# A graph network on one NeuronCore: one gathered tile in four blocks is fetched row by row by SyncE, with addresses from its registers

## The chip, the core and the metric

The kernel runs on one core of a Trainium2 chip, in one launch. The metric is the device time of an execution in microseconds (us), the median of several runs. The program before the change was timed three times: 7339.11, 7335.75 and 7313.08 us, median 7335.75 us. One more execution was profiled.

The engines are called as the profile calls them: PE (matrix multiply; PEld is its weight load), DVE (vector), ACT (scalar), POOL (the engine that issues gathers here) and SP (SyncE, which only issues DMAs). "SPq" is a line of SP's queue. L653 means line 653 of the kernel.

## What is computed

There are 10000 nodes of 512 features and 160000 edges sorted by destination. Layer 0 gives every edge one of four types; layer 1 is two plain neighbourhood averages. Cut to what matters:

```
h   = relu(layernorm(x))
msg = (h @ rel_W[r] + rel_b[r])[src, edge_type]          # one row of 512 per edge
agg = segment_sum(msg, dst) / max(deg, 1)
x1  = layernorm(h + h @ self_W + self_b + agg)
x   = x + layernorm(x1 + gelu(x1 @ W1 + b1) @ W2 + b2)   # layer 0
h   = relu(layernorm(x))
h   = relu(h @ W_self1 + mean(h[src] over edges) @ W_neigh1 + b1)
h   = relu(h @ W_self2 + mean(h[src] over edges) @ W_neigh2 + b2)
out = x + h                                              # layer 1
```

All is float32. What costs time is that a row of 2 KB has to be fetched from DRAM for every edge, three times over: once from the table `hall_d` of all four products of every node, once from `h1_d` and once from `h2_d`.

## The kernel before, in words

Nodes are handled in blocks of 128, one on each partition: 78 full blocks and one last of 16 nodes (`NB` = 79, `full` = 78). The program has four passes, which follow each other.

**Pass 1** (`products`, L597) normalises x, multiplies it by the five weight matrices of layer 0 and stores `hall_d`. Beside it a generator, `edges` (L562), works out on DVE which rows each block needs. It yields between its steps, and `products` resumes it once a block. `lists` (L391) writes index tables that stay in SBUF.

**The index tables.** A node's first T = 11 incoming edges are its own lanes: gather t of block b takes for partition p the t-th edge of node p (`row`), and the gathered tile is simply added to the block's sum. The edges beyond the eleventh are packed, 128 to a tile, and each block has five such tiles (`orow`, `OT` = 5). What does not fit in these goes to tiles shared by several blocks: one for every 4 blocks and one for every 16 (`SPANS` = (4, 16), L80). `srow[0]` and `srow[1]` (L127) hold their row numbers, one column for a tile, 128 partitions deep; `share` (L534) fills a column once the last block of its span has been looked up. Which node a packed row belongs to is in `loc`; `hots` (L666) turns that into 0/1 matrices with which PE adds the rows to the right partitions.

**Passes 2, 3 and 4** (`aligned`, L636) loop over the blocks in the order 78, 0, 1, ..., 77. The order of instructions on each engine is that in which they are written (`manual_schedule`). For every block:

- `gather` (L649) has POOL issue one indirect DMA for each tile, 128 rows of 2 KB: at every fourth block the tile of 4 blocks and at every sixteenth that of 16 (L658 to L660, called `tail0` and `tail1`, two buffers each), then five `orow` tiles, then eleven `row` tiles. The last sixteen share a ring of 28 buffers (`RING`, L640).
- `sums` (L674) has PE add the seven packed tiles into a PSUM tile `pa`, through the 0/1 matrices. The order (L678) begins with `tail1`, then `tail0`, then the five `orow` tiles; matmuls are at L680.
- `add` (L688) has DVE add the eleven `row` tiles to `pa`, one by one (L692).

`begin` (L684) is gather and sums for the next block, called while the current one is worked on. So POOL runs ahead of PE and DVE until the ring is full, and a ring buffer comes free when PE or DVE has used it.

Pass 2 (loop from L903) then normalises the block and gives it to a two-matrix MLP that is done by groups of four blocks, spread over the following iterations (`Group.parts`). SP loads `xs` (L719, two blocks at a time) and `xr` (L725) and stores `h1` (L859) and `xn` (L878). Passes 3 and 4 (loop from L1004) are the two averages: ACT scales the sum, PE transposes it and multiplies by two matrices (L1018, L984), DVE adds bias and residual. SP loads `hb`, 1 MB for four blocks (L970), in pass 4 also `res` (L973), and stores `ob` (L997), also 1 MB for four blocks. SP issues nothing else there, and it waits in the order of the program: a load that needs a buffer or a store that needs a result holds up what is behind it.

Between passes 2 and 3, L944 shifts all row numbers right by two, from rows of `hall_d` (node and type) to rows of `h1_d` and `h2_d` (node).

The functions the change touches:

Of the kernel before, what the change touches and what calls it, by code (L numbers as in the profile page):

```python
# [8 lines left out]
F32 = mybir.dt.float32  # L9
F32R = mybir.dt.float32r  # L10
BF16 = mybir.dt.bfloat16
I32 = mybir.dt.int32
# [9 lines left out]
def kernel(  # L22
# [101 lines left out]

    row = const.tile([P, full, T], I32, name="row")
    orow = const.tile([P, NB, OT], I32, name="orow")
    srow = [const.tile([P, -(-full // n)], I32, name=f"srow{i}") for i, n in enumerate(SPANS)]  # L127
    loc = const.tile([P, NB, OT + NL], F32, name="loc")
    fits = const.tile([1, 1], I32, name="fits")
# [261 lines left out]
    def lists(ep, ep2, pse, found):  # L391
# [166 lines left out]
        while ahead:  # L558
            look_up(*ahead.pop(0))
            yield  # L560

    def edges(ep, ep2, pse):  # L562
        found = {k: ep.tile([P, NB], F32, name=f"f_{k}") 
# [72 lines left out]
    def aligned(ctxa):  # L636
# [8 lines left out]
            return min(P, N - b * P)  # L645

        tails = [None] * NL

        def gather(b, table):  # L649

            def rows(n, idx, name="rows", bufs=RING):
                t = gat.tile([P, D], F32, name=name, bufs=bufs)
                nc.gpsimd.indirect_dma_start(  # L653
                    out=t[:n], out_offset=None, in_=table,
                    in_offset=bass.IndirectOffsetOnAxis(ap=idx, axis=0))
                return t[:n]

            for lv, n in enumerate(SPANS):  # L658
                if b < full and b % n == 0:
                    tails[lv] = rows(P, srow[lv][:, b // n:b // n + 1], f"tail{lv}", 2)  # L660
            others = [rows(P, orow[:, b, t:t + 1]) for t in range(OT if b < full else OT_LAST)]
            if b < full:
                others += tails
            return others, [rows(P, row[:, b, t:t + 1]) for t in range(own(b))]
# [9 lines left out]
        def sums(b, others, hot):  # L674

            r, n = height(b), len(others)
            pa = psA.tile([P, D], F32, name="pa")
            order = list(range(n)) if b == full else list(range(OT, n))[::-1] + list(range(OT))  # L678
            for t in order:
                nc.tensor.matmul(pa[:r], hot[:, t, :r], others[t], start=(t == order[0]),  # L680
                                 stop=(t == order[-1]))
            return pa
# [12 lines left out]
        with ExitStack() as s:  # L695
# [209 lines left out]
            for bs in plan:  # L905
                for b in bs:
                    r = height(b)
                    if b == bs[0]:
                        before, grp = grp, Group(bs)
                    if i + 2 < len(blocks):  # L910
                        load(blocks[i + 2])
                    if i + 1 < len(blocks):
                        hot = hots(blocks[i + 1])
                    got = second()
                    pa, mine = held
                    add(b, pa, mine)
                    v = nodes[b]
                    nc.vector.scalar_tensor_tensor(v[:r], pa[:r], rdeg[:r, b:b + 1], v[:r],
                                                   op0=OP.mult, op1=OP.add)
                    first = (b, now.stats(v[:r], r))  # L920
                    part = products(queue.pop(0) if queue else [], turning)
                    next(part)
                    now.finish()
                    scaled(got, first)
                    next(part, None)
                    if i + 1 < len(blocks):
                        held = begin(blocks[i + 1], hot, table)

                    if b == bs[0] and before:
                        queue += before.parts()  # L930
                    turning = lambda g=grp, b=b, v=v: g.turn(b, v)
                    i += 1
# [8 lines left out]
                next(part, None)  # L941


        for t in (row, orow, *srow):  # L944
            nc.vector.tensor_scalar(t, t, R.bit_length() - 1, None, op0=OP.logical_shift_right)
        quads = [[full]] + [rest[i:i + 4] for i in range(0, full, 4)]
        place = {b: (q, c) for q, bs in enumerate(quads) for c, b in enumerate(bs)}
        for step, (h_d, ws, wn, bs) in enumerate(((h1_d, ws1, wn1, bs1), (h2_d, ws2, wn2, bs2))):
            with ExitStack() as s:
                wp = s.enter_context(tc.tile_pool(name="wp3", bufs=1))  # L950
                ip = s.enter_context(tc.tile_pool(name="ip", bufs=2))
                psT = s.enter_context(tc.tile_pool(name="psT3", bufs=3, space=PSUM))
                psO = s.enter_context(tc.tile_pool(name="psO3", bufs=3, space=PSUM))
                wss = wp.tile([P, KC, D], F32, name="wss")
                wns = wp.tile([P, KC, D], F32, name="wns")
                nc.sync.dma_start(wss, ws.rearrange("(k p) n -> p k n", p=P))
                nc.sync.dma_start(wns, wn.rearrange("(k p) n -> p k n", p=P))
                bss = wide(wp, bs, D, "bss")
                hbs, ress, outs, hTs = {}, {}, {}, {}

                def quad(t, q, name, bufs):

                    b, n = quads[q][0], len(quads[q])
                    return (ip.tile([P, 4, D], F32, name=name, bufs=bufs)[:height(b), :n],
                            rows_of(t, (b, n, height(b))))

                def load(q):
                    if q < len(quads):
                        hbs[q], at = quad(h_d, q, "hb", 2)
                        nc.sync.dma_start(hbs[q], at)  # L970
                        if step:
                            ress[q], at = quad(xn_d, q, "res", 3)
                            nc.sync.dma_start(ress[q], at)  # L973

                def turn(b):
                    q, c = place[b]
                    hTs[b] = ip.tile([P, KC, P], F32, name="hTb")
                    transposed(psT, hTs[b][:, :, :height(b)], hbs[q][:, c, :], height(b))

                def finish(b, po, mT):  # L980
                    r = height(b)
                    q, c = place[b]
                    for k in range(KC):
                        nc.tensor.matmul(po[:r], mT[:, k, :r], wns[:, k, :], start=False,  # L984
                                         stop=(k == KC - 1))
                    if c == 0:
                        outs[q] = quad(out if step else h2_d, q, "ob", 2)
                    o = outs[q][0][:, c, :]
                    if step:
                        nc.vector.tensor_tensor(po[:r], po[:r], bss[:r], op=OP.add)  # L990
                        nc.vector.scalar_tensor_tensor(o, po[:r], 0.0, ress[q][:, c, :],
                                                       op0=OP.max, op1=OP.add)
                    else:
                        nc.vector.tensor_tensor(o, po[:r], bss[:r], op=OP.add)  # L994
                        nc.scalar.activation(o, o, AF.Relu)
                    if b == quads[q][-1]:
                        nc.sync.dma_start(outs[q][1], outs[q][0])  # L997

                load(0)
                load(1)  # L1000
                turn(blocks[0])
                before = None
                held = begin(blocks[0], hots(blocks[0]), h_d)
                for i, b in enumerate(blocks):  # L1004
                    r = height(b)
                    q, c = place[b]
                    if q and c == 0:
                        load(q + 1)
                    if i + 1 < len(blocks):
                        hot = hots(blocks[i + 1])  # L1010
                    pa, mine = held
                    add(b, pa, mine)
                    m = ip.tile([P, D], F32, name="mb")
                    nc.scalar.activation(m[:r], pa[:r], AF.Copy, scale=rdeg[:r, b:b + 1])  # L1014
                    po = psO.tile([P, D], F32, name="po3")
                    hT = hTs.pop(b)
                    for k in range(KC):
                        nc.tensor.matmul(po[:r], hT[:, k, :r], wss[:, k, :], start=(k == 0),  # L1018
                                         stop=False)
                    if before:  # L1020
                        finish(*before)
                    if i + 1 < len(blocks):
                        turn(blocks[i + 1])
                        held = begin(blocks[i + 1], hot, h_d)
                    mT = ip.tile([P, KC, P], F32, name="mTb")
                    transposed(psT, mT[:, :, :r], m[:r], r)
                    before = (b, po, mT)
                finish(*before)
# [308 lines left out]
```

## Time and profile before

| what | value |
|---|---|
| median of the three runs | 7335.75 us |
| the profiled execution: its own time | 7342.91 us |
| its span, first to last instruction | 7341.1 us |
| POOL busy in the span | 3792.5 us, 52%, 3927 instructions |
| PE / DVE / ACT busy | 77% / 50% / 14% |
| DMA queue of POOL (q0) | 308768 packets, 1008.91 MB, 46.5% of 16 engines' span |
| DMA queue of SP (q1) | 134034 packets, 262.10 MB, 10.1% |
| pass 1 | 0 to 1612 us |
| pass 2, first to last gather | 1612 to 3498 us |
| rest of the MLP, then pass 3, first to last gather | 3498 to 3621; 3621 to 5447 us |
| pass 4, first to last gather, then the end | 5479 to 7308; to 7341 us |

A page of such a profile has the busy time of each engine, the span in 40 slices, the DMA queues, the chain of work that ended last, and the costliest groups of instructions. "Busy" leaves out register, branch, semaphore and DMA-issuing instructions, so SP has no busy time at all and its work is to be seen only in the timeline of its queue. A group's line gives engine, operation, what it writes and reads, how many there are, their mean in ns, and the idle time of the engine just before them with what ended most of it. "Issue" is idle time that no recorded event explains; "remote" is a wait ended by something that the records don't name.

### The profile page before, as it was taken

The page shows a single profiled execution, that of the slowest core. Times are in us where ns is not written, and L with a number is a line of the kernel's source. Part 1 is how long each engine was busy: PE and PEld are TensorE (multiplying, and loading weights), DVE is VectorE, ACT ScalarE, POOL GpSimd, SP SyncE. Part 2 cuts the span into 40 slices and gives each one's busy share as a digit, 9 for nine tenths or more (in the row PEclk, how much of TensorE's full clock was granted, in tenths as well). Part 3 has the DMA queues.
Part 4 walks back from the last instruction along what each step waited for, and adds up shares of the span by engine and source line. Part 5 has one row for each costly group of instructions (what it writes and reads, how often), then busy time and mean ns, then how long its engine had stood idle before and what let it go on. Part 6 is the DMA issues. An engine that isn't in the chain of part 4 may idle for free.

```text
span 7341.1 us, 49909 instructions
## 1 busy us (share of the span) xinstructions
PE 5665.5 (77%) x14251; PEld 2553.8 (35%) x14251; DVE 3658.8 (50%) x7297; ACT 1016.3 (14%) x1667; POOL 3792.5 (52%) x3927
## 2 busy tenths in 40 slices
PE   6999999986889889899766666766665666666666
PEld 3444444432334334344323332332322333332232
DVE  5347777424666666666334434443333444443444
ACT  1000000002232233233201100110100000000000
POOL 0000000016666666666266666666656666666665
PEclk9999999997999999999878888888887888888888
DMA  3222222236767777777366666666666777777775
GB/s 141 109 97 98 93 104 92 85 135 194 211 205 224 224 221 225 220 227 225 129 198 206 206 209 204 208 204 206 203 196 208 220 216 216 219 217 214 220 219 169
DMA packets 456992, 1361.46 MB, mean 185 GB/s; under 512 B 71746, under 2 KB 71746, under 8 KB 446578
## 3 DMA queue, kind: packets, MB, share of 16 engines
q0 software_dynamic: 308768, 1008.91, 46.5%
q1 hardware_dynamic: 134034, 262.10, 10.1%
q10 hardware_dynamic: 13904, 87.17, 3.0%
q8 instruction: 114, 1.87, 0.1%
q14 instruction: 172, 1.41, 0.1%
HBM read 1150.89 MB, written 207.01 MB: 185 GB/s over the span
## 4 chain that ended last, share of the span: by engine, by line
PE 39%; issue 20%; another core or an unknown queue 17%; ACT 3%; DVE 3%; DMA 1%; POOL 1%; ACTq 0%; POOLq 0%; DVEq 0%; SPq 0%
PE pa L680 11%; PE ph L776 6%; PE pm L613 6%; PE po L787 6%; PE po L984 4%; PE po L1018 4%; DVE pa L692 2%; PE pT L167 1%; POOL rows L653 1%; ACT hTb L168 1%; ACT mTb L168 1%; ACT mb L1014 0%; PE pT L764 0%; ACT hid L778 0%
## 5 line engine op out<-in xcount | busy, mean ns | idle before, releaser
L692 DVE TENSOR_TENSOR pa<-pa,rows 128x512 f32<-128x512 f32 x2574 | 1798.5, 699 | 1002.9 <-issue 689.3
L653 POOL DMA_INDIRECT rows<-h_d,row x1716 | 1663.6, 969 | 929.1 <-issue 428.5
L984 PE MATMUL po<-wns,mTb 128*128 128x512 f32 (+1 forms) x1264 | 704.5, 709 | 587.5 <-issue 310.2
L680 PE MATMUL pa<-rows,hot 128*128 128x512 f32 (+1 forms) x2358 | 1080.7, 605 | 46.1 <-issue 20.6
L653 POOL DMA_INDIRECT rows<-hall_d,row x858 | 849.8, 990 | 504.4 <-issue 193.7
L613 PE MATMUL pm<-wrel,hT 128*128 128x512 f32 (+1 forms) x2528 | 1098.1, 592 | 0.0
L1018 PE MATMUL po<-wss,hTb 128*128 128x512 f32 (+1 forms) x1264 | 700.6, 706 | 475.6 <-ACT hTb L168 387.3
L653 POOL DMA_INDIRECT rows<-h_d,orow x786 | 754.1, 959 | 400.1 <-issue 220.7
L776 PE MATMUL ph<-x1T,w1s 128*128 128x512 f32 (+2 forms) x1344 | 606.1, 605 | 158.9 <-ACT hid L778 111.4
L613 PEld LDWEIGHTS pm<-wrel,hT 128*128 128x128 f32 (+1 forms) x2528 | 477.0, 189 | 605.8 <-issue 595.3
L680 PEld LDWEIGHTS pa<-rows,hot 128*128 128x128 f32 (+1 forms) x2358 | 454.2, 193 | 641.9 <-issue 603.7
L984 PEld LDWEIGHTS po<-wns,mTb 128*128 128x128 f32 (+1 forms) x1264 | 280.8, 228 | 995.9 <-issue 691.6
L653 POOL DMA_INDIRECT rows<-hall_d,orow x393 | 373.1, 949 | 434.8 <-SPq L1333 308.5
L787 PE MATMUL po<-w2s,hid 128*128 128x512 f32 (+1 forms) x1264 | 561.4, 596 | 23.2 <-issue 20.8
L1018 PEld LDWEIGHTS po<-wss,hTb 128*128 128x128 f32 (+1 forms) x1264 | 273.7, 228 | 846.3 <-ACT hTb L168 440.4
L680 PE MATMUL pa<-tail,hot 128*128 128x512 f32 x936 | 457.7, 607 | 53.3 <-issue 49.2
L990 DVE TENSOR_TENSOR po<-po,bss 128x512 f32<-128x512 f32 (+1 forms) x79 | 55.0, 696 | 811.3 <-remote 702.7
L487 POOL DMA_INDIRECT win<-rec_d,at x79 | 74.8, 947 | 727.9 <-issue 637.1
L776 PEld LDWEIGHTS ph<-x1T,w1s 128*128 128x128 f32 x1344 | 263.8, 204 | 470.7 <-issue 332.1
L616 DVE TENSOR_TENSOR ha<-pm,brel 128x512 f32<-128x512 f32 (+1 forms) x316 | 216.4, 687 | 405.1 <-PE pm L613 405.1
L994 DVE TENSOR_TENSOR ob<-po,bss 128x512 f32<-128x512 f32 (+1 forms) x79 | 54.4, 688 | 597.4 <-remote 268.8
L787 PEld LDWEIGHTS po<-w2s,hid 128*128 128x128 f32 (+1 forms) x1264 | 236.2, 190 | 312.5 <-issue 308.0
(233 smaller groups left out, 4171.5 us busy)
## 6 DMA issues: line engine op xcount, KB each, us to landing
hall_d<-ha ACTq DMA_DIRECT2D x78, 1024.0 KB
hb<-h_d SPq DMA_DIRECT2D x38, 1024.0 KB
rows<-h_d,row POOLq DMA_INDIRECT x1716
xs<-xs_d SPq DMA_DIRECT2D x39, 512.0 KB
xr<-xr_d SPq DMA_DIRECT2D x39, 512.0 KB
xn_d<-xr SPq DMA_DIRECT2D x39, 512.0 KB
h_d<-h SPq DMA_DIRECT2D x39, 512.0 KB
xg<-in_x_dram SPq DMA_DIRECT2D x19, 1024.0 KB
```

What stands on the lines that cost most here:

```text
L167: nc.tensor.transpose(p[:, k, :r], rows[:, k * P:(k + 1) * P], ident[:r, :r])
L168: nc.scalar.copy(dest, p[:, :, :r])
L487: nc.gpsimd.indirect_dma_start(out=win[:, c, :], out_offset=None, in_=rec_d, in_offset=bass.IndirectOffsetOnAxis(ap=at[:, c:c + 1], axis=0))
L613: nc.tensor.matmul(pm[:r], hT[:, k, :r], w[:, k, :], start=(k == 0), stop=(k == KC - 1))
L616: nc.vector.tensor_tensor(ha[:r, j - 1, :], pm[:r], brel[:r, (j - 1) * D:j * D], op=OP.add)
L653: nc.gpsimd.indirect_dma_start(out=t[:n], out_offset=None, in_=table, in_offset=bass.IndirectOffsetOnAxis(ap=idx, axis=0))
L680: nc.tensor.matmul(pa[:r], hot[:, t, :r], others[t], start=(t == order[0]), stop=(t == order[-1]))
L692: nc.vector.tensor_tensor(pa[:r], pa[:r], t[:r], op=OP.add)
L776: nc.tensor.matmul(ph[:, :n], w1s[:, k, f * P:(f + 1) * P], self.xT[:, k, :n], start=(k == 0), stop=(k == KC - 1))
L787: nc.tensor.matmul(po[:r], self.hid[:, f, c * r:(c + 1) * r], w2s[:, f, :], start=(f == 0), stop=(f == FC - 1))
L984: nc.tensor.matmul(po[:r], mT[:, k, :r], wns[:, k, :], start=False, stop=(k == KC - 1))
L1018: nc.tensor.matmul(po[:r], hT[:, k, :r], wss[:, k, :], start=(k == 0), stop=False)
```

## The change

Except for the first of a pass, the tiles that four blocks share are no longer gathered by POOL. A transposed copy of `srow[0]`, called `srow_1`, has one tile's 128 row numbers in one partition. It is made at the end of `lists`, by a copy to float, a PE transpose and a copy back to integers, and L944 shifts it with the other tables.

`fetch(b, table)` is called at the head of every iteration of all three loops, after the iteration's `load`. In the four iterations of one span it fetches the tile of the next: each call loads 32 row numbers into 32 registers of SP with one load instruction, and then issues 32 DMAs on SP, one a row, each with its source address computed from a register. A row is written as four pieces of 128 floats. It does nothing for the last, short block and from the span on that doesn't exist. So it works in 76 iterations of each pass, for spans 1 to 19.

`gather` takes the fetched tile instead of gathering one, and `sums` takes `tail1` first, then the five `orow` tiles, and `tail0` last.

```diff
+    srow_1 = const.tile([-(-full // SPANS[0]), P], I32, name="srow_1")
...
         while ahead:
             look_up(*ahead.pop(0))
             yield
+        ns = srow_1.shape[0]
+        srow_f = ep.tile([P, ns], F32, name="srow_f")
+        nc.vector.tensor_copy(srow_f, srow[0])
+        pl = pse.tile([P, 512], F32, name="pe")
+        nc.tensor.transpose(pl[:ns, :P], srow_f, ident)
+        nc.vector.tensor_copy(srow_1, pl[:ns, :P])
...
+        coming = {}
+        regs = [nc.sync.alloc_register(f"row{i}") for i in range(P // SPANS[0])]
+
+        def fetch(b, table):
+
+            span, part = b // SPANS[0] + 1, b % SPANS[0]
+            if b == full or span * SPANS[0] >= full:
+                return
+            if part == 0:
+                coming[span] = gat.tile([P, D], F32, name="tail0", bufs=2)
+            p0 = part * len(regs)
+            nc.sync.load(regs, srow_1[span:span + 1, p0:p0 + len(regs)])
+            for i, reg in enumerate(regs):
+                at = nc.sync.snap(reg, min_val=0, max_val=table.shape[0] - 1)
+                nc.sync.dma_start(
+                    coming[span][p0 + i:p0 + i + 1, :].rearrange("p (c d) -> p c d", c=4),
+                    table[bass.ds(at, 1), :].rearrange("p (c d) -> p c d", c=4))
...
-                    tails[lv] = rows(P, srow[lv][:, b // n:b // n + 1], f"tail{lv}", 2)
+                    tails[lv] = coming.pop(b // n) if b and not lv else rows(P, srow[lv][:, b // n:b // n + 1], f"tail{lv}", 2)
...
-            order = list(range(n)) if b == full else list(range(OT, n))[::-1] + list(range(OT))
+            order = list(range(n)) if b == full else [n - 1, *range(n - 1)]
...
                     if i + 2 < len(blocks):
                         load(blocks[i + 2])
+                    fetch(b, table)
...
-        for t in (row, orow, *srow):
+        for t in (row, orow, srow_1, *srow):
...
                     if q and c == 0:
                         load(q + 1)
+                    fetch(b, h_d)
```

## The prediction, made before the changed kernel ran

> **What bounds the kernel now.** I read the passes' busy times first, then POOL's timeline, then POOL's waits in each pass, and last SP's queue, since the change moves work from POOL to SP. The first view is busy time by stretch, from the first to the last gather of passes 2, 3 and 4.
>
> ```profile
> core 0: us, PE busy (x) PEld busy (x) DVE busy (x) ACT busy (x) POOL busy (x), PEclk, DMA share, GB/s
> 1612.00:3498.00 1886.00, 1601.41 (x3768) 705.52 (x3769) 1177.75 (x1952) 536.10 (x862) 1247.33 (x1275) 0.91 0.72 220
> 3621.00:5446.00 1825.00, 1219.87 (x2931) 546.08 (x2932) 711.37 (x992) 178.10 (x308) 1222.68 (x1275) 0.83 0.69 206
> 5480.00:7307.00 1827.00, 1210.86 (x2932) 542.84 (x2933) 763.29 (x1068) 135.22 (x232) 1238.20 (x1275) 0.81 0.71 217
> ```
>
> A pass has about 1276 gathers in 79 blocks: 23.9 us a block in pass 2 and 23.1 in passes 3 and 4. POOL looks two thirds busy, but its timeline says more:
>
> ```profile
> 6039.58 0.94 POOL L653 DMA_INDIRECT rows<-h_d,row  x1 [0.30 <-issue]
> 6040.82 0.94 POOL L653 DMA_INDIRECT rows<-h_d,row  x1 [0.30 <-issue]
> 6042.07 0.94 POOL L653 DMA_INDIRECT rows<-h_d,row  x1 [0.30 <-issue]
> 6043.32 0.94 POOL L653 DMA_INDIRECT tail<-h_d,srow  x1 [0.30 <-DMA rows<-h_d,row]
> ...
> 6058.30 0.95 POOL L653 DMA_INDIRECT rows<-h_d,row  x1 [0.30 <-issue]
> 6064.77 0.94 POOL L653 DMA_INDIRECT rows<-h_d,row  x1 [5.52 <-remote]
> ```
>
> A gather starts every 1.25 us, 0.95 of it shown busy and 0.30 not. 1276 x 1.25 = 1595 us: POOL issues back to back for 85% of pass 2 and 87% of passes 3 and 4. The rest is stalls like that at 6058, about 290 us in pass 2 and 230 in each of the others, where POOL wants a ring buffer that PE or DVE hasn't freed. POOL's waits in pass 2 (total us, times, longest us) name PE, and PE is busy 1601 of 1886 us there, so pass 2 is nearly as much PE's as POOL's.
>
> ```profile
> POOL rows L653 <- PE pa L680: 141.3, 42, 13.4
> POOL rows L653 <- PE po L787: 41.2, 34, 3.3
> ```
>
> SP's queue, in pass 3 and at the start of pass 2:
>
> ```profile
> 4017.19 0.36 SPq L970 DMA_DIRECT2D hb<-h_d  x1
> 4064.39 0.36 SPq L997 DMA_DIRECT2D h_d<-ob  x1
> 4110.15 0.36 SPq L970 DMA_DIRECT2D hb<-h_d  x1
> ...
> 1611.01 0.36 SPq L140 DMA_DIRECT2D ln1w<-in_L_gnn_ln_w_dram  x1
> 1611.49 0.35 SPq L140 DMA_DIRECT2D lnb<-in_L_gnn_ln_b_dram  x1
> 1611.95 0.36 SPq L741 DMA_DIRECT2D h<-in_L_gnn_b_dram  x1
> ```
>
> SP issues two DMAs in four blocks and waits otherwise. Back to back, one takes 0.36 us and the next starts 0.46 later; over the 100 closest pairs of the trace the spacing is 0.37 to 0.57 us, median 0.41 to 0.45.
>
> **What the Trainium skill says.** "Perfetto Trace Analysis", section "DMA Instruction — HWDGE (DVE, Sync)": the recorded duration of such a DMA is the sequencer's and the descriptor generator's time, without the data. The trace agrees: 0.36 us for an `hb` load whose last landing comes 4.6 to 5 us after issue, with its first packet 1.0 us after issue. So 0.36 is a price for SP's time. "DMA: Bandwidth & Descriptors", section "Why a DMA increments its semaphore by 16 and not by 1": a DMA runs on the largest number of engines, up to 16, that divides its outermost dimension, on SP's path the lowest-numbered ones. A row cut in four would use engines 0 to 3; no run here shows it yet. "Runtime: NRT & Kernel Launch", section "Instruction fetch mechanics": a register load costs about 200 ns a register even in bulk (from HBM, in its account). The trace has only loads of one register, 0.47 us on SP (L1300).
>
> **The change, part by part.** (1) *Removed:* 19 gathers in each of three passes, 57 x 1.25 = 71 us of POOL's time. (2) *Added on SP:* 76 fetches in a pass, each a load of 32 registers and 32 DMAs. The trace shows neither a bulk load nor an address from a register. The load is bounded by 0.47 us (as one register) and 32 x 0.2 = 6.4 us (the page's price); I take 2.5, since a row of one partition ought to come in fewer trips than 32. A row's DMA is bounded below by the closest spacing, 0.41 us, and above by twice that, 0.82, for a few register operations, the bounds of the address and the 12 increments that four engines don't make. I take 0.55. One fetch F is then 2.5 + 32 x 0.55 = 20 us, with ends at 0.5 + 13.1 = 13.6 and 6.4 + 26.2 = 33 us. A block gives 23.1 us (23.9 in pass 2). SP's own DMAs are under 0.5 us a block, and DMAs behind a 1 MB load may wait some 5 us for it, once or twice in four blocks, another 1 to 2 us a block. So SP fits at F = 20 with 1 to 2 us to spare, and stops fitting at F of about 22 to 23, that is 0.62 us a row. Everything hangs on that. (3) *Waits:* a fetch at iteration b stands ahead of that iteration's stores and, in pass 2, of `xr` and the next `xs`; each may come up to 20 us later than now. They hide behind their buffers: `xs` is loaded two blocks ahead, `hb` four, `xr` is used an iteration later. In passes 3 and 4 SP leaves the `ob` store in the middle of iteration b (b divisible by 4), issues three fetches in 60 us, and the last must have landed for the sums in iteration b+3, 69 us after the store: 7 us to spare, allowing 2 for landing. If SP is later, PE waits, and DVE, ACT and POOL's ring behind it. (4) *Order of the matmuls:* `tail0` last costs nothing by itself and gives it five tiles of 2 x 0.43 us, 4 us, more time. (5) *DMA load:* a fetched tile puts 64 KB on each of engines 0 to 3 in place of 16 KB on all; in four blocks an engine carries about 66 x 16 = 1056 KB of gathers, so +4.5% on four engines that are 0.7 busy. Zero to 0.5% of a pass; I take zero. (6) *The transposed table:* one copy, transpose, copy, under 2 us at the end of pass 1, and one shift: zero, since DVE has 2.7 us of idle time before each L616 there; 2 us if not.
>
> The sum, with SP fitting: of 71 us what shows? POOL sets the pace 87% of the time in passes 3 and 4, but a gather saved ahead of a stall can only lengthen the stall. I take half there and a third in pass 2, where PE is close behind: 2 x 24/2 + 24/3 = 32 us, between 0 and 71. The profiled execution took 7342.9 us (span 7341.1), 7 above the median; 7343 - 32 = 7311 there, and 7336 - 32 = 7304 for the median.
>
> **The rivals.** *SP becomes the bound.* For it: 0.62 us a row is only 0.2 above what the trace shows for a fixed address, and the page's register price alone would add 4 us. Against it: 32 rows a block at any spacing that the trace shows fit. Each us of F beyond 23 costs 76 fetches in three passes: 76 x (3F - 70.1), with 70.1 the three periods' sum. F = 26 (0.62 a row and 6.4 for the load) gives 76 x 7.9 = 600 us, so 7336 + 600 = 7936; F = 25 gives 7708, F = 33 gives 9530. It decides from F = 23.4, or from 22 with SP's own work. *SP fits on average but is late in order:* its stores and `tail0` come after POOL has filled the ring. At 0.3 to 0.5 us a block that is 237 blocks x 0.4 = 95, less what POOL saves: about 7400. *POOL's time is hidden:* the stalls are PE's and take all 71 back: 7336. That the rows aren't fetched by SP can't be, by the diff.
>
> **How the numbers follow.** SP fits and some of POOL's time shows: 0.50, 7304, own range 7264 (all 71) to 7345. SP is the bound: 0.33, about 7936. SP late in order: 0.12, 7400. Hidden: 0.05, 7336. Half a per cent, 37 us, is about what a measurement of this kernel can tell from no change, so faster means below 7299. The first case puts 0.27 there, 0.18 within and 0.05 above; with the others faster 0.27, same 0.24, slower 0.49. The low end is 7262. Above 7800, that is F over 25.4, lies about half of the SP-bound case, 0.17.
>
> **What would show it.** POOL's L653 groups should hold 57 fewer gathers at the same 1.25 us. SP's timeline should show runs of 32 issues: their spacing and the gap ahead of each run are the two numbers I had to bound. If a fetch takes under 22 us, SP has gaps and PE's first matmul on `tail0` doesn't wait. If it takes more, SP's queue is solid, the block's period equals the fetch, and POOL's stalls grow to fill it. I am wrong in the mechanism if SP has gaps and the time still rises, and wrong in size if POOL's stalls in passes 3 and 4 stay at 230 us (all of the 71 shows) or grow by 24 (none does).

## The result, and the profile after

The changed kernel takes 9016.86 us (median of four runs, 8995.32 to 9044.25) where the kernel before, timed beside it, takes 7330.53: 1.231 times as long, with a 95% interval of 1.226 to 1.235. It is slower by 1686 us. The profiled execution took 9010.84 us, with a span of 9008.9.

All that follows comes from several chips of the same type, and they are of two kinds. On those of the prediction and on two more the kernel before takes 7330 to 7371 us; on two others it takes 6656 to 6667. I call them the **slow kind** and the **fast kind**. One chip of each kind came up twice, and both kept their kind. A run is compared only with the kernel before on the same chip.

The first view is busy time by stretch again, passes 2, 3 and 4 of the changed kernel, from first to last gather:

```profile
1609.60:3938.00 2328.40, 1605.17 (x3738) 709.13 (x3738) 1174.28 (x1947) 536.82 (x862) 1233.71 (x1257) 0.84 0.59 178
4092.40:6455.90 2363.50, 1198.54 (x2922) 541.89 (x2922) 710.78 (x989) 181.49 (x307) 1209.92 (x1257) 0.75 0.54 159
6522.30:8939.80 2417.50, 1204.50 (x2922) 543.58 (x2922) 763.45 (x1065) 136.69 (x231) 1227.76 (x1257) 0.74 0.55 164
```

POOL has 57 instructions fewer in all (3870, before 3927), 19 gathers a pass, as it should, and yet each pass is 440 to 590 us longer. No engine's busy time grew by more than 4 us a pass, and the DMA queues move less in a microsecond (159 to 178 GB/s where it was 206 to 220). So everything waits. The costliest groups of the page say for what; behind the last bar stand the idle time just before, and what ended most of it. The first line is of the kernel before, the others are of the changed one:

```profile
L680 PE MATMUL pa<-tail,hot 128*128 128x512 f32 x936 | 457.7, 607 | 53.3 <-issue 49.2
...
L717 DVE TENSOR_TENSOR pa<-pa,rows 128x512 f32<-128x512 f32 x2574 | 1798.9, 699 | 3111.1 <-issue 2362.3
L705 PE MATMUL pa<-tail,hot 128*128 128x512 f32 x936 | 540.5, 662 | 2095.0 <-DMA tail<-h_d 1528.7
L678 POOL DMA_INDIRECT rows<-h_d,orow x786 | 757.1, 963 | 1721.5 <-DVE pa L717 1251.8
```

PE's matmuls on the shared tiles wait 2095 us where they waited 53, and all but 3 us of it for SP's rows (1528.7 us for `h_d` in 38 waits, 563.7 for `hall_d` in 19: once a span in each of three passes). DVE waits behind PE, and POOL for the ring buffers that DVE then doesn't free. SP's own waits, in total us, times, longest; the first two are of the kernel before:

```profile
SPq L997 <- DVE ob L991: 777.1, 16, 92.1
SPq L997 <- ACT ob L995: 771.8, 16, 92.1
...
SPq L670 <- DMA tail<-h_d: 41.9, 75, 1.4
...
SPq L1023 <- DVE ob L1017: 35.0, 5, 20.0
```

Before, SP waited 777 and 772 us for the results that it stores; now it waits for hardly anything in these passes. Its queue is solid: a block takes 31.6 us (30.9, 31.6 and 32.3 in the three passes), and SP's fetch is 30.6 of them. SP is the bound. SP's timeline shows its pace (start, us, number of DMAs; the third and the last two lines are narrower windows into the fourth):

```profile
4989.80 6.79 SPq L670 DMA_DIRECT2D tail<-h_d  x16
4996.69 0.40 SPq L996 DMA_DIRECT2D hb<-h_d  x1
5002.91 5.67 SPq L670 DMA_DIRECT2D tail<-h_d  x7
4999.52 27.18 SPq L670 DMA_DIRECT2D tail<-h_d  x32
...
5010.69 6.36 SPq L670 DMA_DIRECT2D tail<-h_d  x4
5008.57 14.92 SPq L670 DMA_DIRECT2D tail<-h_d  x11
```

16 rows go out in 6.79 us, 0.42 a row. Then 32 rows take 27 us: 7 in 5.67 (0.8 each) and 4 in 6.36 (1.6 each). POOL's timeline of the same microseconds has the difference:

```profile
5001.52 0.95 POOL L678 DMA_INDIRECT rows<-h_d,orow  x1 [31.94 <-DVE pa L717]
5002.77 0.95 POOL L678 DMA_INDIRECT rows<-h_d,orow  x1 [0.30 <-issue]
...
5014.05 0.95 POOL L678 DMA_INDIRECT rows<-h_d,row  x1 [0.31 <-issue]
```

While POOL stood still, for 31.94 us up to 5001.52, SP went at 0.42 us a row. When POOL issues gathers back to back, SP slows to a fourth of that pace.

From the records of SP's instructions: a row is three of them, a register operation (44 ns), a move (29 ns) and the DMA (228 ns), and unhindered the next row begins 0.415 us after it. In the slow stretches all three are held up, the register operations too: a row then takes about 0.7, 1.4, 2.1, 2.8, 3.5 or 4.2 us, in steps of 0.7. A row takes 0.46 us on average where POOL is idle, and 1.30 where it issues throughout. A fetch, from its load to the end of its last row, takes 30.6 us on average (30.62): 2.7 for the load and 27.9 for the rows.

### The profile page after: what moved, and what is told of

It reads as the page before. It is cut to its first block, busy times and chain, and to the rows that moved or that the text cites. A ratio compares the mean times of both kernels' runs of the same rounds, so it can differ in the third digit from the quotient of the medians.

```text
span 9008.9 us, 72273 instructions
## 1 busy us (share of the span) xinstructions
PE 5659.7 (63%) x14252; PEld 2564.0 (28%) x14252; DVE 3662.5 (41%) x7300; ACT 1023.2 (11%) x1667; POOL 3750.9 (42%) x3870
## 3 DMA queue, kind: packets, MB, share of 16 engines
q1 hardware_dynamic: 148626, 277.07, 9.1%
## 5 line engine op out<-in xcount | busy, mean ns | idle before, releaser
L705 PE MATMUL pa<-tail,hot 128*128 128x512 f32 x936 | 540.5, 662 | 2095.0 <-DMA tail<-h_d 1528.7
L705 PEld LDWEIGHTS pa<-tail,hot 128*128 128x128 f32 x936 | 173.1, 206 | 2262.9 <-issue 1817.3
L1045 PE MATMUL po<-wss,hTb 128*128 128x512 f32 (+1 forms) x1264 | 626.4, 642 | 96.3 <-ACT hTb L170 62.1
L170 ACT COPY mTb<-pT 128x512 f32<-128x512 f32 (+1 forms) x158 | 92.0, 582 | 2830.4 <-PE pT L169 1550.6
L1045 PEld LDWEIGHTS po<-wss,hTb 128*128 128x128 f32 (+1 forms) x1264 | 251.4, 210 | 368.0 <-issue 300.7
```

Of the source, the lines that this page charges most:

```text
L170: nc.scalar.copy(dest, p[:, :, :r])
```

## The experiments

Theory A: SP is the bound, because its instructions slow down while POOL issues gathers, whatever they do. Its rivals: B, each small DMA costs about 0.9 us; C, the bytes of a fetch crowd one DMA engine. The first four ran on one chip of the slow kind, each of them once (kernel before: 7371 us, one run). A row part is the time from a fetch's first row to its last.

**One instruction a row.** Constant addresses, no load:

```diff
-                at = nc.sync.snap(reg, min_val=0, max_val=table.shape[0] - 1)
+                at = span * P + p0 + i
...
-                    table[bass.ds(at, 1), :].rearrange("p (c d) -> p c d", c=4))
+                    table[at:at + 1, :].rearrange("p (c d) -> p c d", c=4))
```

> The changed kernel, but each of the 32 row DMAs of a fetch has a constant source address (rows of the table in sequence), so that SP has one instruction a row where it had three, and no register load. The number of DMAs, their bytes and the tile that PE waits for stay. It leaves out the choice of the rows: the shared tiles hold other rows than they should. Theory A (SP's pace: while POOL's gathers move data, every SP instruction takes about 0.7 us, whatever it does, so a row of three costs about 2.1 us then and 0.417 us otherwise): 20 us of gathers a block take 28 rows at 0.7, the other 4 at 0.4, a fetch takes about 22 us and fits; 7300 to 7450 us. Theory B (each small DMA costs about 0.9 us in SP's queue or in landing, the register work being cheap): the fetch stays at about 28 us, less the load of 2.7; about 8400 us. Theory C (64 KB a fetch through one DMA engine): as B, 8400 to 9000 us.

Measured: 7350.4 us, a row part of 20.3 us in place of 27.5. As many row DMAs and bytes as in the changed kernel, a third of the instructions, and the loss of 23% is gone. B and C are out as the main cost. The spacing of these rows has its steps too, but nearly all end at two of them, 0.7 and 1.4 us.

**A quarter of the bytes.**

```diff
-                coming[span] = gat.tile([P, D], F32, name="tail0", bufs=2)
+                coming[span] = gat.tile([P, P], F32, name="tail0q", bufs=2)
...
-                nc.sync.dma_start(
-                    coming[span][p0 + i:p0 + i + 1, :].rearrange("p (c d) -> p c d", c=4),
-                    table[bass.ds(at, 1), :].rearrange("p (c d) -> p c d", c=4))
+                nc.sync.dma_start(coming[span][p0 + i:p0 + i + 1, :],
+                                  table[bass.ds(at, 1), :P])
...
```

> The changed kernel, but a row DMA brings only the first 512 bytes of its row, and PE adds the shared tile of four blocks to the first 128 columns only; that matmul is the last but one, not the last. SP's instructions and the number of DMAs stay, the bytes are a quarter. It leaves out three quarters of those tiles' sums. Theory A (SP's pace by instructions): nothing changes, 8950 to 9050 us. Theory B (a cost per DMA): the same. Theory C (bytes through one engine): a fetch falls by at least half of its row part, SP fits, 7300 to 7500 us.

Measured: 9172.1 us, a row part of 28.1 us. The bytes don't matter; C is out.

**Two rows in a DMA.**

```diff
...
-                at = nc.sync.snap(reg, min_val=0, max_val=table.shape[0] - 1)
-                nc.sync.dma_start(
-                    coming[span][p0 + i:p0 + i + 1, :].rearrange("p (c d) -> p c d", c=4),
-                    table[bass.ds(at, 1), :].rearrange("p (c d) -> p c d", c=4))
+                if i % 2:
+                    continue
+                at = nc.sync.snap(reg, min_val=0, max_val=table.shape[0] - 2)
+                nc.sync.dma_start(coming[span][p0 + i:p0 + i + 2, :], table[bass.ds(at, 2), :])
...
```

> The changed kernel, but one DMA brings two neighbouring rows, by the register of the first: 16 DMAs and 48 instructions a fetch in place of 32 and 96, with the same bytes. The row numbers are held two below the table's end. It leaves out the choice of every second row. Theory A (SP's pace): 20 us of gathers take 9.5 DMAs at 2.1 us, the other 6.5 take 2.7 us, the load 2.7: a fetch of about 25 us, or a little less since SP then nearly fits; 7350 to 7800 us. Theory B (a cost per DMA): a fetch of 2.7 + 14 = 17 us, SP fits, 7300 to 7340 us. Theory C (bytes through one engine): 8000 to 9000 us, unless the two rows go to two engines.

Measured: 7578.0 us, a fetch of 23.4 us, 24.7 to 25.6 us a block. A's range holds it, B's doesn't. Half the instructions take three quarters of the time. A reason that fits: POOL then issues during 82% of a fetch and not 66%, so what SP gains lets gathers flow, and these slow SP.

**Fewer gathers.**

```diff
-            return others, [rows(P, row[:, b, t:t + 1]) for t in range(own(b))]
+            few = [rows(P, row[:, b, t:t + 1]) for t in range(0, own(b), 2)]
+            return others, [few[t // 2] for t in range(own(b))]
```

> The changed kernel, but POOL gathers only six of a full block's eleven own lanes; DVE adds each of them twice, the last once, so that its work stays. It leaves out five lanes of the sums. POOL issues 11 to 12 gathers a block in place of 16 to 17, about 14 us in place of 20. Theory A (SP's pace is slow while gathers flow): 14 us of gathers take 6.5 rows, the other 25.5 take 10.6 us, the load 2.5: a fetch of 26 to 27 us, 7800 to 8100 us. Theory B or C (a cost of the row DMAs themselves, 28 us of a fetch whatever POOL does): 8950 to 9050 us.

Measured: 7338.2 us, a fetch of 23.1 us. SP's instructions are those of the changed kernel, and only POOL's changed: the slow pace comes with the gathers. It fell by more than A said. What fits is that POOL's runs of gathers got shorter, 3.5 gathers on average and not 9.7, if a pause of over 0.4 us ends a run: a row gets slower the longer a run has gone on, as the table in the last section has it.

The next four came to a chip of the **fast kind** (kernel before: 6655.6 us). Two were meant for the slow pace, and it wasn't there.

**The own lanes' gathers with a quarter of the bytes.**

```diff
...
-                    out=t[:n], out_offset=None, in_=table,
+                    out=t[:n, :P] if own_lane else t[:n], out_offset=None,
+                    in_=table.rearrange("n (c d) -> (n c) d", c=4) if own_lane else table,
...
-                nc.vector.tensor_tensor(pa[:r], pa[:r], t[:r], op=OP.add)
+                nc.vector.tensor_tensor(pa[:r, :P], pa[:r, :P], t[:r, :P], op=OP.add)
```

> The changed kernel, but POOL's gathers of the own lanes (eleven of a full block's sixteen to seventeen) bring 512 bytes a row in place of 2 KB, and DVE adds them to the first 128 columns only. POOL issues as many gathers with as many rows as before. It leaves out three quarters of these lanes' sums, and the rows are others. SP slows down while gathers run; this asks for what in them. Theory A1 (the bytes in flight): about half the bytes of a block are left, so the traffic while gathers run is near 100 GB/s, where a row took 0.65 us in the changed kernel's trace; a fetch of about 32 x 0.65 + 2.5 = 23 us, and 7250 to 7500 us. Theory A2 (POOL's issuing or the number of rows gathered, not the bytes): a row still takes 1.6 to 1.8 us beside running gathers, a fetch about 30 us, 8700 to 9050 us.

Measured: 6545.3 us, 0.44 us a row although POOL issued all the time. On this chip that decides nothing between A1 (the bytes in flight) and A2 (POOL's issuing).

**The kernel before, thinned.** The edit of the thinned run, without SP's fetches.

> The kernel before, thinned as the changed one was: POOL gathers six of a full block's eleven own lanes, DVE adds each twice, the last once. It leaves out five lanes of the sums. SP fetches no rows. If the thinned changed kernel, at 7338 us and 24.1 us a block, was bound by SP's fetches (theory A), this one has no such bound: POOL needs about 12 x 1.25 = 15 us a block, PE about 20 us in pass 2 and 16 in passes 3 and 4, so 6000 to 6500 us. If it was bound by something else (PE or DVE), this one is at 7250 to 7350 us too.

Measured: 5569.4 us. The expectation was for the slow kind, so it missed, and the thinned changed kernel ran on another chip. It shows only that with 12 gathers a block no other engine holds the time near 7300, on a chip of the fast kind.

**Nothing in place of the gathers.**

```diff
-                if b < full and b % n == 0:
+                if b < full and b % n == 0 and (lv or not b):
```

> The kernel before, with the tile that four blocks share gathered once a pass, at the first block, and used again for all others: 57 gathers fewer, and nothing in their place. It leaves out the right rows of those tiles. This is the most that the change could have brought, with a perfect fetch. If half of POOL's 71 us shows in passes 3 and 4 and a third in pass 2, as step 1 of the prediction has it: 32 us less than the kernel before, a ratio of 0.9956. If all shows: 71 us, 0.990. If POOL's time is hidden behind PE and DVE: 1.000.

Measured: 6590.4 us, 0.9897 of the kernel before (95% interval 0.9881 to 0.9914, as all intervals that follow): 68 us of POOL's 71 show, within 11 us either way.

**Half of the change.**

```diff
-            span, part = b // SPANS[0] + 1, b % SPANS[0]
-            if b == full or span * SPANS[0] >= full:
+            span, part = 2 * ((b + 4) // 8) + 1, (b + 4) % 8
+            if b == full or b < 4 or span * SPANS[0] >= full:
...
```

> Half of the change: SP fetches only every second shared tile (spans 3, 5 to 19), 16 rows a block over the eight blocks ahead of it; POOL gathers the others. It computes what the reference does. 48 row instructions a block, as in the run with pairs of rows, which took 24.7 to 25.6 us a block and 7578 us. Theory A (SP's pace by instructions beside gathers): SP doesn't fit at full gather traffic (16 x 1.7 + 2.5 = 30 us a block) and slows the gathers to about 25 us a block: 7450 to 7650 us. Theory B (a cost of about 0.9 us for each row, whatever runs): 16 x 0.9 + 2.5 = 17 us, SP fits, and half of POOL's saving shows: 7310 to 7340 us.

Measured: 6618.0 us, 0.9936 (0.9920 to 0.9953): a gain here, and 0.52 us a row. Is the slow pace a matter of the chip, or of how many rows SP fetches? The next three came to another chip of the slow kind (kernel before: 7349.4 us).

**The changed kernel, half of the change, and the own lanes' quarter, on the slow kind.**

> The changed kernel itself again, because the last four runs came from a chip on which the kernel before takes 6656 us and not 7336, and on which an SP row took 0.44 to 0.65 us beside gathers of up to 260 GB/s, where it took 1.6 to 1.8 us in the changed kernel's first trace. Theory S (the slow pace of SP's instructions beside gathers belongs to the chip, or to what else goes on on it): where the kernel before takes about 7340 us, the changed one takes 8900 to 9200; where it takes about 6656, a fetch takes 32 x 0.5 + 2.5 = 18 to 20 us, fits in a block of some 21 us just, and the changed kernel takes 6580 to 6800 us. Theory K (the slow pace comes with this kernel's 32 rows a block, on any chip): 20% or more above the kernel before, whatever that takes.

Measured: 9112.3 us, 1.238 (1.233 to 1.244).

> Half of the change again (every second shared tile by SP, 16 rows a block). Theory S: where the kernel before takes about 7340 us, SP's 48 row instructions don't fit beside full gathers and it takes 7450 to 7650 us; where it takes 6656, 0.9936 of it as measured. Theory K: about 0.994 of the kernel before on any chip.

Measured: 7580.1 us, 1.030 (1.026 to 1.034), where the same kernel gave 0.9936 on the other kind. Theory S holds: the slow pace belongs to the chip, and not to the 32 rows a block.

> The changed kernel with the own lanes' gathers bringing 512 bytes a row, added to 128 columns only; three quarters of these lanes' sums are left out, and the rows are others. On the chip with the fast pace it took 6545 us. On one with the slow pace: theory A1 (bytes in flight slow SP) 7250 to 7500 us, theory A2 (POOL's issuing or the number of gathered rows) 8700 to 9050 us.

Measured (one run): 9102.3 us, a fetch of 31.1 us, a row at 1.35 us beside issuing. In pass 4 the queues moved less than 100 GB/s all told:

```profile
6540.00:8960.00 2420.00, 1205.06 (x2920) 545.32 (x2921) 428.93 (x1060) 142.10 (x236) 1183.36 (x1220) 0.74 0.30 93
```

The bytes of the gathers are not what slows SP. A2 was right, 50 us above its range.

The next four ran on the same chip again (kernel before: 7359.6 us).

**The changed kernel, and nothing in place of the gathers.**

> The changed kernel once more, as the measure for the other runs of this call. Where the kernel before takes about 7340 us: 9000 to 9150 us, as on two chips of three so far. Where it takes about 6656 us: theory S (the slow pace belongs to the chip) says that a fetch fits at 16 to 20 us a block, and 6580 to 6800 us; theory K (32 rows a block bring the slow pace on any chip) says 8000 us or more.

Measured: 9076.0 us, 1.234 (1.231 to 1.237).

> The kernel before with the tile of four blocks gathered only once a pass (57 gathers fewer, nothing in their place; it leaves out the right rows of those tiles). On the chip where the kernel before takes 6656 us this was 0.9897 of it, 68 us, nearly all of 57 x 1.25 = 71. Where it takes 7340: POOL's stalls of 230 to 290 us a pass are there to take part of it back. Step 1 of the prediction: 32 us, 0.9956. All of it: 0.990. None: 1.000.

Measured: 7272.5 us, 0.9887 (0.9867 to 0.9907): 83 us by this ratio, with an interval of 68 to 98 that holds all of POOL's 71.

**Half as many rows in a gather.**

```diff
-            return others, [rows(P, row[:, b, t:t + 1]) for t in range(own(b))]
+            return others, [rows(64, row[:64, b, t:t + 1]) for t in range(own(b))]
...
-            r = height(b)
+            r = min(64, height(b))
```

> The changed kernel, but each gather of an own lane (eleven of sixteen to seventeen a full block) brings 64 rows in place of 128, and DVE adds them on 64 partitions. The number of gathers stays, the gathered rows fall by a third, to about those of the thinned run (1400 a block, where that had 1470). It leaves out these lanes' sums for half of the nodes. On a chip of the slow kind: if the gathered rows slow SP down (theory D), a fetch falls as in the thinned run, to about 24 us, and the time to 7200 to 7500 us; if the number of gathers that POOL issues does (theory I), a fetch stays at 30 to 32 us, 8900 to 9150 us. On a chip of the fast kind: about 6550 us by both.

Measured (one run): 9160.4 us, a row at 1.37 us beside issuing. Fewer rows and fewer bytes don't help, fewer gathers do: it goes with POOL's issuing (theory I, again a little above its range).

**One instruction a row, with more runs.**

> The changed kernel with constant row addresses, one SP instruction a row and no register load; the shared tiles hold other rows than they should. It took 7350.4 us beside one run of the kernel before at 7371.1. On a chip of the slow kind, theory A (SP's pace by instructions): SP needs 23.6 to 24.9 us a block, about what a block has, so POOL's saving is mostly taken back: a ratio of 0.994 to 1.004. On a chip of the fast kind SP has time to spare, and the ratio comes near that of the run without these gathers: 0.989 to 0.993.

Measured: 7367.0 us, 1.0007 (0.9997 to 1.0018). One instruction a row lets SP just keep up, at 23.5 to 24.9 us a block, and takes back all of the 83 us.

The last three ran on two chips of the fast kind (kernel before: 6666.9 us on a new one, then 6655.9 on that of the first runs of this kind).

**The changed kernel on the fast kind.**

> The changed kernel again. Where the kernel before takes about 7340 us: 9000 to 9150 us, as on all chips so far where it did. Where it takes about 6656: theory S (the slow pace belongs to the chip) 6580 to 6800 us, theory K (32 rows a block bring it on any chip) 8000 us or more.

Measured: 6594.2 us (two runs), 0.989 (0.9872 to 0.9909): **the whole change gains 1.1% on a chip of the fast kind.** Its passes, SP's timeline, and PE's matmuls on the shared tiles:

```profile
1608.30:3237.80 1629.50, 1554.04 (x3814) 685.10 (x3815) 1192.91 (x1986) 543.38 (x877) 1244.42 (x1257) 0.98 0.81 255
3340.10:4942.40 1602.30, 1264.17 (x2981) 537.16 (x2982) 721.15 (x1009) 176.43 (x312) 1219.24 (x1257) 0.89 0.77 236
4960.00:6567.40 1607.40, 1251.35 (x2980) 533.22 (x2981) 774.53 (x1086) 136.45 (x235) 1223.98 (x1257) 0.89 0.79 248
```

```profile
4994.39 10.28 SPq L670 DMA_DIRECT2D tail<-h_d  x25
5004.77 0.34 SPq L1023 DMA_DIRECT2D out_dram<-ob  x1
5007.53 27.29 SPq L670 DMA_DIRECT2D tail<-h_d  x59
```

```profile
L705 PE MATMUL pa<-tail,hot 128*128 128x512 f32 x936 | 506.5, 624 | 77.6 <-DMA tail<-h_d,srow 48.8
```

1257 gathers at 1.25 us are 1571 of 1602 to 1630 us: POOL issues almost without a pause. Beside that SP puts 59 rows and a load into 27.29 us, in a pass that moves 248 GB/s. A fetch takes 17.7 us, a block 20.4 to 20.8. PE waits 78 us where it waited 2095, and 49 of the 78 are for shared tiles that POOL gathers (`srow`), not for SP's rows.

**A fourth of the change**, eight rows a block over sixteen blocks:

```diff
-            span, part = b // SPANS[0] + 1, b % SPANS[0]
-            if b == full or span * SPANS[0] >= full:
+            span, part = 4 * ((b + 4) // 16) + 3, (b + 4) % 16
+            if b == full or b < 12 or span * SPANS[0] >= full:
...
```

> A fourth of the change: SP fetches only the shared tiles of spans 7, 11, 15 and 19, eight rows a block over the sixteen blocks ahead of each; POOL gathers the others. It computes what the reference does. 12 gathers fewer, at the 87/57 = 1.5 us that one was worth on the chip of the slow kind: 18 us. Theory A (SP's pace by instructions, 1.6 to 2.1 us a row beside gathers): 8 x 1.9 + 2.5 = 18 us a block fit in 23, and the 18 us show in part: a ratio of 0.997 to 1.000. If SP's rows hold back POOL or the stores even where they fit (theory H): above 1.002.

Measured: 6642.5 us, 0.9966 (0.9953 to 0.9978).

> A fourth of the change again (spans 7, 11, 15 and 19 by SP, eight rows a block). It gave 0.9966 on a chip where the kernel before takes 6667 us. Where it takes about 7340: theory A (SP's pace by instructions, 1.6 to 2.1 us a row beside gathers): 18 us a block fit in 23, 0.997 to 1.000. Theory H (SP's rows hold back POOL or the stores even where they fit): above 1.002.

Measured: 6638.6 us, 0.9976 (0.9965 to 0.9987). Both came to the fast kind, so whether a fourth of the change gains on the slow kind was not tried. On the fast kind a fourth, a half and the whole gave 0.997 to 0.998, 0.994 and 0.989, and the whole is the best there. On the slow kind the two that were tried, half and whole, both lose.

## Why the prediction was wrong

**The step that failed is (2), the price of a row.** It took 0.55 us, bounded by 0.41 and 0.82. On the chips of the slow kind a row took 0.89 us on average: 0.46 with POOL idle, 1.3 beside its gathers. The load was right (2.5 said, 2.7 measured). That is 0.08 us a register, less than half of the 0.2 that the Trainium skill, "Runtime: NRT & Kernel Launch", section "Instruction fetch mechanics", has for loads that in its account come from HBM; so the upper end of 6.4 us was far off. So F was 30.6 us and not 20, and SP did not fit. On the fast kind the same rows took 0.46 us and F was 17.7: there the step and its conclusion hold. The register operations, for which 0.55 left room, cost next to nothing when nothing holds them up (0.415 us a row); what was missing is the dependence on POOL.

The flaw was in the choice of the evidence. The lower bound came from the 100 closest pairs of SP's DMAs, which are by selection the unhindered ones. And the upper bound, twice that, added instructions but no dependence on what POOL was doing, while a fetch lies beside gathers most of its time. The trace of before had the warning, on PE. These are transposes of one tile, for which no record shows anything to wait for between them:

```profile
6001.65 0.27 PE L167 MATMUL pT<-ident,mb 128*128 128x128 f32 x1
6002.92 0.27 PE L167 MATMUL pT<-ident,mb 128*128 128x128 f32 x1 [1.00 <-issue]
6005.72 0.37 PE L167 MATMUL pT<-ident,mb 128*128 128x128 f32 x1 [2.53 <-issue]
6008.51 0.37 PE L167 MATMUL pT<-ident,mb 128*128 128x128 f32 x1 [2.42 <-issue]
```

Each takes 0.3 us, yet they start up to 2.8 us apart, by "issue", a wait for nothing that is recorded. It is not the rule: of 474 such pairs of transposes, 79 start more than 0.7 us apart, the others mostly 0.11. An engine whose simple instructions come at times at a tenth of their pace should have made me ask what SP's would do.

**The rival came true as it was written.** "SP becomes the bound" priced F at 76 x (3F - 70.1). With F = 30.62 that is 1654 us; measured 1686. The formula was right and the F put into it, 26, too small. That the two agree so closely is in part luck: 0.1 us of F is 23 us, and the formula leaves out SP's own DMAs. The range ended at F = 25.4, though the prediction's own bounds of F reached 33.

**(1), POOL's saving.** It happened (57 gathers fewer), but its visible part was under-sized. I let stalls take back half to two thirds and took 32 us. With nothing in place of the gathers, 83 us show on the slow kind and 68 on the fast. POOL's waits on the slow kind, first in the kernel before, then in that run:

```profile
POOL rows L653 <- remote: 372.6, 129, 7.5
POOL rows L653 <- PE pa L680: 187.6, 55, 13.4
...
POOL rows L653 <- remote: 364.2, 129, 7.3
...
POOL rows L653 <- PE pa L680: 179.6, 47, 14.3
```

The stalls stayed. A gather saved ahead of a stall did not lengthen the stall. That is the outcome that the prediction itself had put at "all of the 71 shows".

**(3), waits in SP's order.** They cost nothing where SP fits. On two chips of the fast kind the change gave 0.989 and the run without these gathers 0.9897, with intervals of about 12 us to either side, which leaves little room for late stores.

**(4), the order of the matmuls,** wasn't tried alone; the same comparison leaves it little.

**(5), DMA load.** The cost of zero was right as far as the run with a quarter of the bytes tells, for the wrong picture. A row isn't four pieces for four engines. SP's queue has 148626 packets where it had 134034, two for each of the 7296 rows: one of 2 KB and one of 4 bytes. The four pieces were joined into one, and the instruction's record says so too: one element of 2048 bytes. The section of the Trainium skill that the prediction draws on here ("DMA: Bandwidth & Descriptors", "Why a DMA increments its semaphore by 16 and not by 1") goes by the shape "as the instruction carries it", and that agrees with one piece.

**(6), the table:** zero, as said; the first gather of pass 2 comes at 1609.6 us, where it came at 1612.

**What stays open.** What slows the instructions on the slow kind isn't settled. It is neither the bytes of SP's rows, nor the bytes or the rows of the gathers, nor SP's waits. It goes with POOL's issuing, and it differs between chips of one type. Something like it reaches PE too: in the kernel without the shared gathers 85 of the 474 pairs of transposes start over 0.7 us apart on the slow kind, and none on the fast kind.

The records hold a rival that no run tested. Six steps of 0.7 us, the most that nearly all rows take, are one for each start and each end of a row's three instructions; nearly all rows of one instruction end at two steps, and 2.8 us between PE's transposes would be four, for a weight load and a transpose. And of the rows that take 1 to 2.4 us in the changed kernel, 47% show their DMA as lasting under 30 ns, where it takes 228 unhindered. So it may be the writing of a time stamp that is held up, and the instruction with it. Every execution of the experiments left a recorded span; no run shows how an unrecorded one would go.

The kernel without the shared gathers also shows what else differs between the kinds, with no rows on SP. First the slow kind, then the fast, the same matmul group with its idle time:

```profile
L1018 PE MATMUL po<-wss,hTb 128*128 128x512 f32 (+1 forms) x1264 | 700.7, 706 | 408.3 <-ACT hTb L168 356.0 <-issue 52.2
```

```profile
L1018 PE MATMUL po<-wss,hTb 128*128 128x512 f32 (+1 forms) x1264 | 570.7, 594 | 0.0
```

On the fast kind this idle time is gone, and so are POOL's "remote" stalls: its passes take 1606 to 1632 us, not 1801 to 1874. That this is the same slowness is argued, not shown: the granted clock of PE differs too, 0.885 against 0.933 in these two runs.

## What to carry to other kernels

Moving work to an idle queue is priced by that queue's pace beside the work that stays, not by its closest records: 0.42 us a row became 0.89 here, and a block time of 23 us was overrun by a fetch of 31. Where a change fits by one or two microseconds, look first for simple instructions that come late by "issue" on any engine, and count instructions and not DMAs: one a row just fitted, three lost 23%. And measure on more than one chip: the same change took 1.23 times as long on one kind and 0.989 on the other.

## What the runs showed of the hardware

The spacing of SP's rows against the time since POOL began to issue without a pause of over 0.4 us, from the records (medians, us):

| POOL has issued for | changed, slow kind | thinned gathers, slow kind | changed, fast kind |
|---|---|---|---|
| under 1.25 us | 0.42 | 0.42 | 0.42 |
| 2.5 to 5 us | 0.71 | 0.65 | 0.42 |
| 5 to 7.5 us | 1.43 | 0.78 | 0.42 |
| 7.5 to 10 us | 2.11 | 2.11 | 0.42 |
| 30 to 60 us | 3.50 | 4.20 | 0.42 |

On the slow kind a row gets slower in steps of about 0.7 us the longer POOL issues, and in the changed kernel the median is back at 0.42 from 1.25 us after POOL stops. That looks like something that fills and drains; what it is, no run showed. As the spacings stand in steps, a median can jump by one where few cases change. The last row has few cases (54, 14 and 223), the first rows of the fast kind fewer still (1 to 6), since POOL hardly ever stops there.

A load of 32 registers from one partition took 2.7 us on average in the changed kernel on the slow kind and 2.9 on the fast, 1.9 to 4.8 us in nine cases of ten.
